# Cross-attention on one core: the score matrix A built from 11 block products of 64 rows, whose blocks VectorE adds, in place of 12

## The chip, the core and the metric

The kernel runs on one core of a Trainium2 chip. The metric is the device time of one execution in microseconds (us), the median of several runs. TensorE (PE in the profile) multiplies matrices into PSUM banks, VectorE (DVE) and ScalarE (ACT) read PSUM, GpSimd (POOL) works on SBUF, and SyncE (SP) issues the transfers. The order of the instructions on each engine is written out by hand: every engine does its work in the order in which the program names it, and waits where an operand is not ready.

## The reference

x has 16 batches of 256 rows and 256 columns, the context c 16 batches of 77 rows and 192 columns. There are 8 heads. All numbers are float32.

```
Q = x @ Wq,  K = c @ Wk,  V = c @ Wv          (8 heads of 256)
score = Q K^T / sqrt(256), masked             (16 x 8 x 256 x 77)
attn  = softmax(score)
out   = concat over heads (attn V) @ Wo + x
out   = layernorm(out) * gamma + beta
```

## The kernel before

The projections are folded. Once, at the start, the kernel forms for each head G = Wk Wq^T / 16 (192 x 256, in tiles gA for the first 128 context columns and gB for the other 64) and U = Wv Wo (tiles uA, uB). For a group of four batches and a pair of heads it then needs A = G^T c^T (256 x 77 for each head and batch, tile a), and for each batch VW = c U (tile vw). The scores of 128 rows of x (a "tile" t, two for each batch) are x A, and the output is attn VW.

A is prepared two heads at a time by `prepare_a` (L165): part A multiplies with the 128 context rows of gA and cA (L190), part B with the 64 rows of gB and cB, two heads at once on the two halves of the array's rows (L202). Four PSUM banks of 308 columns hold the result, and ScalarE copies them to SBUF (`copy_out`, L966). Seen in 64 rows of context, half of the 256 output rows (dc) and two of the four batches, a head takes 3 x 2 x 2 = 12 block products.

The main loop (L980) runs over batches; in iteration b it makes the scores of batch b+1 (L300), the softmax of it, the product attn VW of batch b, and the layer norm of batch b-1:

- TensorE: scores of two tiles; in every second iteration (those with odd b) the preparation of VW for two batches and of A for two pairs of heads; then `seven(b)` (L435 to L474), the product attn VW by seven block products.
- VectorE: `shift` (L317, adds the bias and takes the minimum, 16 instructions), the second normalisation of the older batch, a transposition, `finish` (L505, L508) and the reciprocals (L353), the first normalisation (L547, L576), `turn` (L369), the transposition of x (L162), and `add_product` (L497), which adds the product in PSUM to x.
- ScalarE: 16 exponentials (L338), the copies of VW and A (L966), the two small steps of `spread` (L526, L527) that give the norm's factor rstd, and the copy of four of the seven products (L473).
- GpSimd: `weigh` (L359), `differences` (L412), `sums` (L429 to L432) and `add_seven` (L483). At the start it also makes the bias (L596 to L598), the sums of uA and uB (L905, L906) and small copies (L638, L642, L643).

All PSUM tiles share one ring of eight banks: a new tile takes the bank of the tile eight places earlier, and its first matmul waits until that one's reader is done.

One row in the profile with "x32" counts 32 matmul instructions: each float32 matmul of the program is two instructions, and four of 32 output columns run side by side in the array, so that 8 instructions of 128 rows, or 16 of 64 rows, are one step of the stream.

Of the kernel before, what the change touches and what calls it, by code (L numbers as in the profile page):

```python
# [16 lines left out]
P = 128  # L17
H = 8
# [9 lines left out]
def kernel(  # L28
# [78 lines left out]
    bet = const.tile([P, DI], F32, tag="bet", name="bet")  # L107
    xg_of = {}

    x_rows = x.rearrange("b (t p) d -> p (b t) d", p=P)  # L110
# [8 lines left out]

    def load_x(g, n=None, of=QT):  # L120
        if not n:
            xg_of[g] = const.tile([P, GT, DI], F32, tag=f"xg{g}", name=f"xg_{g}")
        lo, hi = (0, GT) if n is None else (n * QT, n * QT + of)
        nc.sync.dma_start(xg_of[g][:, lo:hi], x_rows[:, g * GT + lo : g * GT + hi, :])

# [15 lines left out]

    def load_xT(g, lo=0, hi=GT, after_pool=False):


        if lo == 0:
            xT_of[g] = in_two("xT", [P, GT * NM, 2, BK], g)
        if after_pool:
            nc.gpsimd.memset(xT_of[g][:BK, lo * NM, 0, :1], 0.0)
        rows = x.rearrange("b s d -> (b s) d")[(g * GT + lo) * P : (g * GT + hi) * P, :]
        rows = rows.rearrange("(m r) (i n) -> i r m n", r=BK, i=NM)  # L150
        for i in range(NM):
            nc.sync.dma_start(
                xT_of[g][i * BK : (i + 1) * BK, lo * NM : hi * NM].rearrange(
                    "p m n q -> p m (n q)"
                ),
                rows[i],
            )

    def transpose_x(g, j):

        cols = xT_of[g][:, j * NM : (j + 2) * NM]
        nc.vector.transpose(cols, cols)  # L162


    def prepare_a(g, places, lo=0, hi=GB, rest_first=False):  # L165
# [46 lines left out]

        return part_A, part_B, copies

    def prepare_vw(b, rest_first=False):
# [77 lines left out]
    def scores(t):  # L293
        g = t // GT
        j, bl = t % GT, (t // QT) % GB
        ps = [ps_mm.tile([P, 512], F32, tag="mm", name=f"ps_{t}_{a}") for a in range(2)]
        for m in range(NM):
            for dc in range(2):
                for i in range(NM):
                    nc.tensor.matmul(  # L300
                        ps[m // 2][i * BK : (i + 1) * BK, m % 2 * 2 * S2 : (m % 2 + 1) * 2 * S2],
                        xT_of[g][:, j * NM + m, dc],
                        flat(a_of[g][:, dc, bl, 2 * i : 2 * i + 2, :]),
                        start=(dc == 0),
                        stop=(dc == 1),
                    )
        ps_of[t] = ps
# [24 lines left out]
    def exponential(t):  # L332
        e = sp.tile([P, H, S2], F32, tag="e", name=f"e_{t}")
        s, top = s_of.pop(t)
        den = st.tile([P, H], F32, tag="den", name=f"den_{t}")
        for h in range(H):
            one = slice(h, h + 1)
            nc.scalar.activation(  # L338
                e[:, h],
                s[:, h],  # L340
                AF.Exp,
                bias=top[:, one],
                scale=-1.0,
                accum_out=den[:, one] if summed_by_act(t) else None,
            )
        e_of[t] = e, den

# [128 lines left out]
    def add_seven(b):  # L476

        m = m_of.pop(b)
        j = QT * b % GT
        y = xg_of[QT * b // GT][:, j : j + QT].rearrange("p t (c d) -> p t c d", c=2)  # L480

# [13 lines left out]
    def add_product(t):  # L495
        y = xg_of[t // GT][:, t % GT, :]
        nc.vector.tensor_tensor(y, po_of.pop(t), y, ALU.add)  # L497

    def finish(t):
        if t in po_of:  # L500
            add_product(t)
        g, j = t // GT, t % GT
        y = xg_of[g][:, j, :]
        bn = st.tile([P, 6], F32, tag="bn", name=f"bn_{t}")
# [5 lines left out]
    def finish_halves(t):  # L510
        g, j = t // GT, t % GT
        bn = st.tile([P, 2, 6], F32, tag="bn2", name="bn_halves", bufs=1)
        for c, po in enumerate(po_of.pop(t)):
            y = xg_of[g][:, j, c * P : (c + 1) * P]
            nc.vector.tensor_tensor(y, po, y, ALU.add)
            nc.vector.bn_stats(bn[:, c], y)
# [28 lines left out]
    def centre(t):  # L545
        y = xg_of[t // GT][:, t % GT, :]
        nc.vector.scalar_tensor_tensor(  # L547
# [3 lines left out]
    def store(t):  # L551
        nc.sync.dma_start(out_rows[:, t, :], xg_of[t // GT][:, t % GT, :])

    def scale_and_store(t):
# [3 lines left out]
        rstd, _ = rstd_of.pop(t)  # L558
        y = xg_of[t // GT][:, t % GT, :]
        nc.scalar.activation(y, y, AF.Identity, scale=rstd)  # L560
# [3 lines left out]
    def normalise(t, aside=False, centred=False):  # L564

        g, j = t // GT, t % GT
        rstd, less = rstd_of.pop(t)
        y = xg_of[g][:, j, :]
        if aside:
# [11 lines left out]
        if t ^ 1 in done:  # L581
            t |= 1
            j |= 1
            nc.sync.dma_start(
                out_rows[:, t + 1 - QT : t + 1, :], xg_of[g][:, j + 1 - QT : j + 1, :]
            )

# [14 lines left out]
    with tc.tile_pool(name="wonce", bufs=1) as wp:  # L602
# [54 lines left out]

        qT_03 = const.tile([P, 2, 4, DI], F32, tag="xg0", name="qT_03")
        qT_12 = const.tile([P, 2, 4, DI], F32, tag="xg1", name="qT_12")
        kT_03 = const.tile([P, 2, 4, DL], F32, tag="xg2", name="kT_03")  # L660
        kT_12 = const.tile([P, 2, 4, DL], F32, tag="xg3", name="kT_12")
        qT = qT_03[:, 0].rearrange("p (e dc) d -> p e dc d", e=2)
        kT = kT_03[:, 0].rearrange("p (e dc) l -> p e dc l", e=2)
        qT_blk = {1: qT_12[:, 0], 2: qT_12[:, 1], 3: qT_03[:, 1]}
        kT_blk = {1: kT_12[:, 0], 2: kT_12[:, 1], 3: kT_03[:, 1]}
        for a in range(1, NF):
# [22 lines left out]
        def load_late():  # L689
# [3 lines left out]
            for a in range(NF):  # L693
                nc.sync.dma_start(wo_of[a // 2][:, a % 2], wo_rows[a])
            load_xT(0, 0, QT)
            load_bias(0, GB)
            load_rest()
            load_xT(0, QT, GT)
            load_bias(GB, B)
# [22 lines left out]
        def turn_k():  # L722
            pt = ps_mm.tile([P, 4, P], F32, tag="mm", name="pt_k")
            for n in range(4):
                nc.tensor.transpose(pt[:, n], wk_nat[:, n * P : (n + 1) * P], ident)
            nc.scalar.copy(kT_03[:, 0, :, :P], pt)

# [161 lines left out]
        for a in range(1, NF):  # L889
# [18 lines left out]
        for j in range(NF // 2):  # L908
# [3 lines left out]
            if j:  # L912
                transpose_x(0, 0)
                bias_of(0, GB)
# [36 lines left out]


    def work_of(b, rest_first=False):
        g, n = b // GB + 1, b % GB
        work = [prepare_vw(b, rest_first)]
        if g < NG - 1 or g == NG - 1 and n < NF // 2:
            work.append(prepare_a(g, (n,), rest_first=rest_first))
        elif b <= NS:
            part = (0, 2) if g < NG else (2, GB)
# [10 lines left out]
    def turn_x_and_normalise(g, n, old):  # L970
        to_turn = (g, 0) if g < NG and n == 2 else (g - 1, GT // 2) if g > 1 and n == 0 else None
        if to_turn:
            for j in range(to_turn[1], to_turn[1] + GT // 2, 2):
                transpose_x(to_turn[0], j)
        if old:
# [4 lines left out]
    for b in range(-1, B - 1):  # L980
# [17 lines left out]
        works = work_of(b + 1) if alone or n % 2 == 0 else []  # L998
        for part_A, _, _ in works:
            part_A()  # L1000
        for _, part_B, _ in works:
            part_B()
        if b == B - 2:
# [17 lines left out]
        for i, t in enumerate(new if b >= 0 else ()):  # L1021
# [3 lines left out]
            weigh(t)  # L1025
        ahead = works and not alone
        if old and not ahead:
            spread(old[0], old[-1] + 1)
        if ahead:
            copy_out(works)  # L1030
            if old:
                spread(old[0], old[-1] + 1)
            works = work_of(b + 2, rest_first=True)
            for _, part_B, _ in works:
                part_B()
            for part_A, _, _ in works:
                part_A()
        copy_out(works)
        if b + 1 < NS:
            differences(b + 1)  # L1040
        if ahead and g < NG:
            load_xT(g, n * QT, (n + 1) * QT, after_pool=True)
        if b < NS:
            if now:
                seven(b)
            if old:
                invert(old[0], old[-1] + 1)
                normalise(old[0])
            for t in new:
                turn(t)  # L1050
            if b < 0:
                for j in range(QT, GT, 2):
                    transpose_x(0, j)
                bias_of(GB, B)
            if alone or ahead:
                turn_x_and_normalise(g, n, old)
                if ahead and g < NG:
                    load_xT(g, (n + 1) * QT, (n + 2) * QT)
            else:
# [61 lines left out]
```

## Time and profile before

| what | value |
|---|---|
| median of 3 runs | 270.72 us (270.66 to 272.16) |
| profiled execution, first to last instruction (span) | 269.2 us |
| what lies around the span, median less span | 1.5 us |
| TensorE busy | 262.9 us, 98% of the span |
| GpSimd busy | 173.2 us, 64% |
| VectorE busy | 185.2 us, 69% |
| ScalarE busy | 157.7 us, 59% |
| granted TensorE clock | 1.000 over the span |

No separate time of the profiled execution itself is given beside its span, so sums that are made in the span are set against the median by the 1.5 us around it. "Busy" is the share in which at least one instruction of the engine ran; idle time of an engine costs something only where another one waits for it.

### The profile page before, as it was taken

The numbers are of one execution on the slowest core, as the hardware profiler recorded it, in microseconds if no ns is written. First come the engines' busy times: TensorE is split into PE (matmuls) and PEld (weight loads), VectorE is DVE, ScalarE is ACT, GpSimd is POOL, SyncE is SP. The second block draws the span as 40 slices with busy tenths as digits, with TensorE's granted clock in tenths as the row PEclk, the third lists the DMA queues.
The fourth block names the chain that finished last, engine by engine and source line by source line (L and its number), as shares of the span: only waits on it lengthen the run. The fifth ranks groups of instructions, "written<-read, shape, count | busy, mean of one in ns | idle before, by whom it ended". The sixth has DMA issues, their size and how long they took to land.

```text
span 269.2 us, 14427 instructions
## 1 busy us (share of the span) xinstructions
PE 262.9 (98%) x6090; PEld 194.3 (72%) x6090; DVE 185.2 (69%) x808; ACT 157.7 (59%) x667; POOL 173.2 (64%) x240
## 2 busy tenths in 40 slices
PE   8999999999999999999999999999999999999993
PEld 7566598954985599459954995499769967984662
DVE  1555966483574758764896379647977897799785
ACT  3243335626857555964587377738684595636772
POOL 1042005637399647995699759965999799685462
PEclk9999999999999999999999999999999999999999
DMA  6999999901500130323022400340044010100112
GB/s 193 200 204 206 325 144 171 322 9 32 130 7 2 41 82 5 69 82 94 5 62 70 110 6 14 108 123 4 6 119 122 2 44 5 44 22 22 44 41 80
DMA packets 41616, 22.69 MB, mean 84 GB/s; under 512 B 24064, under 2 KB 40528, under 8 KB 41552
## 3 DMA queue, kind: packets, MB, share of 16 engines
q1 hardware_dynamic: 41168, 20.98, 32.7%
q0 software_dynamic: 384, 0.79, 1.4%
q8 instruction: 48, 0.79, 1.2%
q14 instruction: 16, 0.13, 0.2%
HBM read 17.57 MB, written 4.19 MB: 81 GB/s over the span
## 4 chain that ended last, share of the span: by engine, by line
PE 93%; DMA 3%; DVE 1%; SPq 1%; issue 0%; DVEq 0%
PE ps L300 25%; PE pa L190 12%; PE pv L224 11%; PE po L448 11%; PE pm L448 8%; PE pa L202 6%; PE pv L235 6%; PE po L381 4%; PE pu L777 3%; PE pr L260 2%; PE pgb L838 2%; DMA c_sb<-in_ctx_dram 2%; DMA wk_blk<-in_L_xattn_Wk_dram 2%; PE pw L791 1%; PE phb L854 1%; PE pr L271 1%
## 5 line engine op out<-in xcount | busy, mean ns | idle before, releaser
L338 ACT ACTIVATE e<-s,top 128x77 f32<-128x77 f32 x256 | 85.3, 346 | 44.5 <-DVE top L317 38.2
L300 PE MATMUL ps<-a,xT 128*32 128x154 f32 x2048 | 70.1, 294 | 0.0
L300 PEld LDWEIGHTS ps<-a,xT 128*32 128x32 f32 x2048 | 66.5, 110 | 1.1 <-issue 0.4
L359 POOL TENSOR_TENSOR p<-e,rden 128x512 f32<-128x512 f32 x64 | 47.5, 768 | 29.5 <-DVE rden L353 29.4
L317 DVE CUSTOM_DVE_ANT_0 s<-ps,bias 128x77 f32<-128x77 f32 x256 | 43.6, 232 | 14.8 <-PE ps L300 14.8
L338 ACT ACTIVATION_READ_ACCUMULATOR e<-s,top 128x1 f32 x224 | 42.0, 187 | 0.0
L190 PE MATMUL pa<-cA,gA 128*32 128x308 f32 (+1 forms) x576 | 36.8, 395 | 0.0
L190 PEld LDWEIGHTS pa<-cA,gA 128*32 128x32 f32 x576 | 19.0, 110 | 20.4 <-issue 6.7
L483 POOL TENSOR_TENSOR xg<-xg,m 128x256 f32<-128x256 f32 x39 | 28.7, 736 | 6.6 <-DVE xg L497 4.6
L576 DVE SCALAR_TENSOR_TENSOR xg<-xg,rstd,bet 128x256 f32<-128x256 f32 x27 | 22.2, 821 | 14.7 <-ACT rstd L527 13.3
L224 PE MATMUL pv<-uA,cA 128*32 128x512 f32 x256 | 30.8, 595 | 0.0
L412 POOL TENSOR_TENSOR ts<-vw 128x768 f32<-128x768 f32 x13 | 24.0, 1848 | 5.9 <-ACT vw L966 5.9
L369 DVE STREAM_TRANSPOSE pT<-p 128x640 f32<-128x640 f32 x32 | 25.5, 820 | 3.4 <-POOL p L359 3.3
L966 ACT COPY vw<-pv 128x512 f32<-128x512 f32 x32 | 17.8, 584 | 15.3 <-PE pv L224 8.1
L497 DVE TENSOR_TENSOR xg<-po,xg 128x256 f32<-128x256 f32 x31 | 11.5, 405 | 14.5 <-PE po L448 13.9
L317 DVE DVE_READ_ACCUMULATOR2_ANT top<- 128x1 f32 x256 | 20.8, 81 | 0.0
L202 PE MATMUL pa<-cB,gB 64*32 64x308 f32 (+2 forms) x512 | 20.4, 387 | 0.0
L966 ACT COPY a<-pa 128x308 f32<-128x308 f32 (+1 forms) x56 | 18.9, 395 | 1.9 <-PE pa L190 0.4
L202 PEld LDWEIGHTS pa<-cB,gB 64*32 64x32 f32 (+1 forms) x512 | 11.0, 110 | 11.4 <-issue 6.2
L547 DVE SCALAR_TENSOR_TENSOR xg<-xg,mv,gam 128x256 f32<-128x256 f32 x30 | 17.5, 585 | 0.1
L235 PE MATMUL pv<-uB,cB 64*32 64x512 f32 x256 | 17.3, 597 | 0.0
L224 PEld LDWEIGHTS pv<-uA,cA 128*32 128x32 f32 x256 | 8.0, 109 | 12.5 <-issue 9.5
(119 smaller groups left out, 407.6 us busy)
## 6 DMA issues: line engine op xcount, KB each, us to landing
xT<-in_x_dram SPq DMA_DIRECT2D x52, 64.0 KB, 2.4
xg<-in_x_dram SPq DMA_DIRECT2D x6, 512.0 KB, 4.2
out_dram<-xg SPq DMA_DIRECT2D x11, 256.0 KB, 2.3
wo<-in_L_xattn_Wo_dram SPq DMA_DIRECT2D x4, 512.0 KB, 8.9
wq_blk<-in_L_xattn_Wq_dram SPq DMA_DIRECT2D x12, 128.0 KB, 4.5
out_dram<-xg SPq DMA_DIRECT2D x10, 128.0 KB, 1.7
wk_blk<-in_L_xattn_Wk_dram SPq DMA_DIRECT2D x12, 96.0 KB, 4.3
xg<-in_x_dram SPq DMA_DIRECT2D x1, 1024.0 KB, 7.9
```

The source lines that it names most:

```text
L190: nc.tensor.matmul(flat(o[i * BK : (i + 1) * BK]), gA[:, h, cols(dc, i)], flat(cA[:, batches, :]), start=not rest_first and n in opening, ...
L202: nc.tensor.matmul(flat(banks[j + k][i * BK : (i + wide) * BK]), gB[half(k), h // 2, dc * P + i * BK : dc * P + (i + wide) * BK], flat(cB[ ...
L224: nc.tensor.matmul(pv[k][i * BK : (i + 1) * BK], cA[:, b, k * BK : (k + 1) * BK], uA[:, parts, :, i], start=not rest_first, stop=rest_first,)
L235: nc.tensor.matmul(pv[k][i * BK : (i + 1) * BK], cB[half(k), b, k * BK : (k + 1) * BK], uB[half(k), parts, :, i], start=rest_first, stop=n ...
L300: nc.tensor.matmul(ps[m // 2][i * BK : (i + 1) * BK, m % 2 * 2 * S2 : (m % 2 + 1) * 2 * S2], xT_of[g][:, j * NM + m, dc], flat(a_of[g][:, ...
L317: nc.vector.tensor_tensor_reduce(s[:, h], ps[a][:, k * S2 : (k + 1) * S2], bias[:, b, :], scale=-1.0, scalar=FAR, op0=ALU.add, op1=ALU.min ...
L338: nc.scalar.activation(e[:, h], s[:, h], AF.Exp, bias=top[:, one], scale=-1.0, accum_out=den[:, one] if summed_by_act(t) else None,)
L359: nc.gpsimd.tensor_tensor(part, e_mh[:, :, :, keys], rden_mh.unsqueeze(3).to_broadcast(list(part.shape)), ALU.mult,)
L369: nc.vector.transpose(pT_of[t].rearrange("p n m q -> p m n q"), p.rearrange("p m (n k) -> p m n k", k=BK),)
L448: nc.tensor.matmul(out[i * BK : (i + 1) * BK], weight[:, i], moving, start=first and n == 0, stop=final and n == len(terms) - 1,)
L483: nc.gpsimd.tensor_tensor(to, to, what, ALU.add)
L966: nc.scalar.copy(dst, src)
```

## The change

For the pairs of heads of groups 1 and 2 and two of the four pairs of group 3 (ten pairs, prepared in iterations b = -1, 1, 3, 5 and 7, where `quick` is true), `prepare_a` is replaced by `prepare_fast`. Of the three blocks of 64 context rows the first two are multiplied by a scheme of seven block products in place of eight (sums of blocks of G and c take the place of the blocks); the third block adds four more. Each is a product of 64 rows and 154 columns, and two heads' products run at once on the two halves of the rows: 11 such steps for a pair of heads.

- The sums of the blocks are made once by GpSimd: `sums_of_g` after the last pair of G, 14 instructions of 64 partitions and 512 elements; `sums_of_c(1, 2)` ahead of the sum of uB; `differences_of_c` and `sums_of_c(2, 4)` after the first two `weigh`.
- For each head one bank "mids" and one bank "ends" of three times 154 columns. The first product of a "mids" bank is copied by ScalarE, and the next product is added onto it in the same place. VectorE then puts the blocks together by four additions that read PSUM (`put_together`); ScalarE no longer copies these parts of A.
- In a quick iteration TensorE makes both batches' VW first (both parts A, then both parts B), then the two pairs of heads, then `seven`. VectorE's additions stand after the two `turn` and ahead of the transposition of x and the second normalisation. The first `put_together` is ahead of the second `turn`.
- The tiles of x (xg) and of the turned x (xT) hold two batches and not four, x in a ring of four and xT in a ring of three, and the exponentials are written in place of the shifted scores. The order of their transfers is the same. The K weights that are turned at the start share the space of the sums of G.

The parts of the diff that the prediction speaks of (the rest changes only the names of the smaller tiles):

```diff
+    HB = GB // 2
+    KX = HB * S2
+    FAST = NG - 1
+    low, high = slice(0, LB), slice(LB, P)
+    cT = const.tile([P, 4, FAST, KX], F32, tag="cT", name="cT")
+    cD = const.tile([P, FAST, KX], F32, tag="cD", name="cD")
+    gC = const.tile([P, NF, P], F32, tag="gC", name="gC")
...
+    def load_x(k):
+        xg_of[k] = const.tile([P, PT, DI], F32, tag=f"xg{k % 4}", name=f"xg_{k}")
+        nc.sync.dma_start(xg_of[k], x_rows[:, k * PT : (k + 1) * PT, :])
...
+            xT_of[k] = pools[0].tile([P, PT * NM, 2, BK], F32, tag="xT", name=f"xT_{k}", bufs=3)
...
+    def sums_of_g():
+        parts = gA.rearrange("p (u e) (i dc c) -> p dc e u i c", e=2, dc=2, c=BK)
+        sums = gS.rearrange("p n (u e) (i c) -> p n e u i c", e=2, c=BK)
+        for e, own, other in ((0, high, low), (1, low, high)):
+            s1, s2, s3 = (sums[own, n, e] for n in range(3))
+            s4 = sums[other, 0, e]
+            nc.gpsimd.tensor_copy(s1, parts[other, 1, e])
+            add(s1, s1, parts[own, 1, e])
+            subtract(s2, s1, parts[own, 0, e])
+            subtract(s3, parts[own, 0, e], parts[own, 1, e])
+            nc.gpsimd.tensor_copy(s4, s2)
+            subtract(s4, parts[other, 0, e], s4)
+            nc.gpsimd.tensor_copy(gC[own], gB[other, :, P:])
+    def halves_of(c, lo, hi):
+        groups = c[:, lo * GB : hi * GB].rearrange("p (g y b) k -> p y g (b k)", y=2, b=HB)
+        return groups[:, 0], groups[:, 1]
+    def sums_of_c(lo, hi):
+        xs, ys = halves_of(cA, lo, hi)
+        t1, t2, t3, t4 = (cT[:, n, lo - 1 : hi - 1] for n in range(4))
+        subtract(t1, ys, xs)
+        for own, other in ((low, high), (high, low)):
+            nc.gpsimd.tensor_copy(t2[own], ys[other])
+        subtract(t3, t2, ys)
+        subtract(t2, t2, t1)
+        for own, other in ((low, high), (high, low)):
+            nc.gpsimd.tensor_copy(t4[own], t2[other])
+        subtract(t4, xs, t4)
+    def differences_of_c(lo, hi):
+        subtract(cD[:, lo - 1 : hi - 1], *halves_of(cB, lo, hi))
...
+    def prepare_fast(g, u):
...
+        for e, h in enumerate(heads):
+            for banks in (mids, ends):
+                banks.append(ps_mm.tile([P, 3, KX], F32, tag="mm", name=f"pf_{g}_{h}_{len(ends)}"))
...
+        def middle(e):
+            h, own = heads[e], (high, low)[e]
+            return [
+                ((mids[e], 2), from_g(own, h, 0), c_of(cA, own, xs)),
+                ((mids[e], 0), from_s(own, 0, h), t_of(own, 0)),
+                ((mids[e], 2), from_s(own, 1, h), t_of(own, 1)),
+                ((mids[e], 1), from_s(own, 2, h), t_of(own, 2)),
+                (
+                    (mids[e], 1),
+                    lambda i: gC[own, u, i * BK : (i + 1) * BK],
+                    c_of(cB, own, ys),
+                ),
+            ]
+        def outer(e):
+            h, own = heads[e], (low, high)[e]
+            return [
+                ((ends[e], 0), from_g(own, h, 0), c_of(cA, own, xs)),
+                ((ends[e], 1), from_s(own, 0, h), c_of(cA, own, ys)),
+                ((ends[e], 2), from_g(own, h, 1), t_of(own, 3)),
+                ((ends[e], 0), from_rest(h, 0), c_of(cB, own, xs)),
+                ((ends[e], 1), from_rest(h, 0), c_of(cB, own, ys)),
+                ((ends[e], 2), from_rest(h, 1), cD[own, g - 1]),
+            ]
+        def pairs():
+            o, m = outer(0), middle(1)
+            ones = o[:2] + m[:1] + o[2:] + m[1:]
+            o, m = outer(1), middle(0)
+            return list(zip(ones, m[:1] + o[:3] + m[1:] + o[3:]))
+        def products():
+            total = {id(bank): 6 for bank in ends} | {id(bank): 5 for bank in mids}
+            lone = {id(bank): e for e, bank in enumerate(mids)}
+            seen = dict.fromkeys(total, 0)
+            for pair in pairs():
+                flags = []
+                for (bank, _), _, _ in pair:
+                    key = id(bank)
+                    n, seen[key] = seen[key], seen[key] + 1
+                    one = key in lone and n == 0
+                    flags.append(
+                        (one or n == (key in lone), one or n == total[key] - 1, one)
+                    )
+                for i in range(NM):
+                    for ((bank, n), weight, moving), (start, stop, _) in zip(pair, flags):
+                        nc.tensor.matmul(
+                            bank[i * BK : (i + 1) * BK, n],
+                            weight(i),
+                            moving,
+                            start=start,
+                            stop=stop,
+                        )
+                for ((bank, n), _, _), (_, _, one) in zip(pair, flags):
+                    if one:
+                        nc.scalar.copy(blocks[lone[id(bank)]][:, 0], by_batch(bank)[:, n])
+        def plus(out, *of):
+            nc.vector.tensor_tensor(out, *of, ALU.add)
+        def put_together(e):
+            mid, end, of = by_batch(mids[e]), by_batch(ends[e]), blocks[e]
+            plus(of[:, 3], mid[:, 2], of[:, 0])
+            plus(of[:, 1:3], mid[:, 0:2], of[:, 3:4].to_broadcast([P, 2, HB, S2]))
+            plus(of[:, 3], mid[:, 0], of[:, 2])
+            plus(of[:, 0:3], end, of[:, 0:3])
+        return products, put_together
...
-        e = sp.tile([P, H, S2], F32, tag="e", name=f"e_{t}")
...
-                e[:, h],
+                s[:, h],
...
+        gS = const.tile([P, 3, H, P], F32, tag="gS", name="gS")
+        sums_of_g()
         load_x(0)
+        load_x(1)
         nc.sync.dma_start(gam, gamma.partition_broadcast(P))
...
         turn_rest_last()
+        sums_of_c(1, 2)
         sum_of(uB)
         for t in range(QT):
             exponential(t)
             weigh(t)
+        differences_of_c(1, NG)
+        sums_of_c(2, NG)
...
+    def fast(b):
+        return b < B - GB - GB // 2
...
-            load_x(g, n, 2 * QT)
+            load_x((g * GB + n) // 2)
...
+        ahead = not alone and n % 2 == 0
+        quick = ahead and fast(b + 1)
...
+        if quick:
+            works += work_of(b + 2)
+            for part_A, *_ in works:
+                part_A()
+            for _, part_B, _ in works:
+                part_B()
+            copy_out(works[:1])
+            products, put_together = prepare_fast(g, n)
+            products()
+            copy_out(works[1:])
...
+        if quick:
+            if old:
+                spread(old[0], old[-1] + 1)
+            if b < 0:
+                for t in new:
+                    turn(t)
+                for t in range(QT, GT, 2):
+                    transpose_x(t)
+            next_products, next_together = prepare_fast(g, n + 1)
+            next_products()
...
+            elif not quick:
+                for t in new:
+                    turn(t)
+            if quick:
+                for e, t in enumerate(new):
+                    if b >= 0:
+                        turn(t)
+                    put_together(e)
+                for e in range(2):
+                    next_together(e)
```

More of the change, by code (lines that the diff above doesn't have):

```diff
@@ L118, in half, with x_of @@
         return slice(i * LB, (i + 1) * LB)
[L120 to L124, printed above, removed]
+    def load_x(k):
+        xg_of[k] = const.tile([P, PT, DI], F32, tag=f"xg{k % 4}", name=f"xg_{k}")
+        nc.sync.dma_start(xg_of[k], x_rows[:, k * PT : (k + 1) * PT, :])
+    def x_of(t, n=1):
+        return xg_of[t // PT][:, t % PT : t % PT + n]
     evacs = [0]
@@ L213, in prepare_a @@
         return part_A, part_B, copies
+    add, subtract = (
+        partial(nc.gpsimd.tensor_tensor, op=op) for op in (ALU.add, ALU.subtract)
+    )
[12 more added lines that the diff above has]
+            nc.gpsimd.tensor_copy(gC[own], gB[other, :, P:])
@@ L656, in pair_in_order @@
             return parts[::-1] if a == 1 else parts
[L658 to L665, printed above, removed]
+        qT_blk = [const.tile([P, 4, DI], F32, tag=f"xg{a}", name=f"qT_{a}") for a in range(NF)]
+        kT_all = const.tile([P, NF, 4, DL], F32, tag="gS", name="kT_all")
+        kT_blk = [kT_all[:, a] for a in range(NF)]
+        qT = qT_blk[0].rearrange("p (e dc) d -> p e dc d", e=2)
+        kT = kT_blk[0].rearrange("p (e dc) l -> p e dc l", e=2)
         for a in range(1, NF):
@@ L725, in turn_k @@
                 nc.tensor.transpose(pt[:, n], wk_nat[:, n * P : (n + 1) * P], ident)
-            nc.scalar.copy(kT_03[:, 0, :, :P], pt)
+            nc.scalar.copy(kT_blk[0][:, :, :P], pt)
         def turn_k_last():
@@ L955, in work_of @@
         work = [prepare_vw(b, rest_first)]
-        if g < NG - 1 or g == NG - 1 and n < NF // 2:
-            work.append(prepare_a(g, (n,), rest_first=rest_first))
-        elif b <= NS:
+        if b <= NS and not fast(b):
             part = (0, 2) if g < NG else (2, GB)
@@ L997 @@
         alone = b + 1 >= B - GB // 2
[L998 to L1002, printed above, removed]
+        ahead = not alone and n % 2 == 0
+        quick = ahead and fast(b + 1)
+        works = work_of(b + 1) if alone or ahead else []
+        if not quick:
+            for part_A, *_ in works:
+                part_A()
+            for _, part_B, _ in works:
+                part_B()
         if b == B - 2:
@@ L1025 @@
             weigh(t)
[L1026 to L1030, printed above, removed]
+        if quick:
+            works += work_of(b + 2)
+            for part_A, *_ in works:
+                part_A()
+            for _, part_B, _ in works:
+                part_B()
+            copy_out(works[:1])
+            products, put_together = prepare_fast(g, n)
+            products()
+            copy_out(works[1:])
+        elif not alone or old:
+            if ahead:
+                copy_out(works)
             if old:
                 spread(old[0], old[-1] + 1)
[L1033 to L1038, printed above, removed]
+            if ahead:
+                works = work_of(b + 2, rest_first=True)
+                for _, part_B, _ in works:
+                    part_B()
+                for part_A, *_ in works:
+                    part_A()
+        if not quick:
+            copy_out(works)
+        if quick:
[8 more added lines that the diff above has]
+            next_products()
         if b + 1 < NS:
@@ L1048 @@
                 normalise(old[0])
-            for t in new:
-                turn(t)
             if b < 0:
-                for j in range(QT, GT, 2):
-                    transpose_x(0, j)
                 bias_of(GB, B)
+            elif not quick:
[8 more added lines that the diff above has]
+                    next_together(e)
             if alone or ahead:
```

81 lines of the change are left out of this document (51 added, 30 removed).

## The prediction, made before the result was known

> **What bounds the kernel now.** I read the page's first part, then the chain of waits, then the timeline of VectorE over one pair of iterations, then the sums by stretch of time.
>
> ```profile
> PE 262.9 (98%) x6090; PEld 194.3 (72%) x6090; DVE 185.2 (69%) x808; ACT 157.7 (59%) x667; POOL 173.2 (64%) x240
> ```
>
> TensorE is busy for nearly the whole span. The chain of waits (start, length, engine, tile and line, number of instructions) says the same: from 13 to 264 us it never leaves TensorE for long. These are rows of it, among them the quick iteration b = 3, which starts at 104.09.
>
> ```profile
> 28.34 1.04 PE pa L202 x16
> ...
> 46.83 5.82 PE pr L260 x32
> ...
> 55.66 1.85 PE pv L224 x16
> ...
> 71.66 1.75 PE pm L448 x64
> ...
> 104.09 4.19 PE ps L300 x128
> 108.28 1.72 PE pv L224 x16
> 110.00 2.07 PE pa L190 x32
> 112.07 1.02 PE pv L235 x16
> 113.09 1.04 PE pa L202 x32
> 114.13 0.86 PE pv L235 x16
> 114.99 1.04 PE pa L202 x32
> 116.02 1.85 PE pv L224 x16
> 117.88 2.07 PE pa L190 x32
> 119.95 1.75 PE pm L448 x64
> 121.70 2.17 PE po L448 x64
> ...
> 187.74 4.19 PE ps L300 x128
> ```
>
> A pair of heads costs TensorE 2.07 + 1.04 = 3.11 us, and no row here waits for another engine. But how far is the next engine from being the bound? VectorE over the same stretch (start, length, line; in brackets the idle time before and what ended it):
>
> ```profile
> 106.90 0.22 DVE L317 CUSTOM_DVE_ANT_0 s<-ps,bias 128x77 f32<-128x77 f32 x1
> ...
> 115.99 0.64 DVE L576 SCALAR_TENSOR_TENSOR xg<-xg,rstd,bet 128x256 f32<-128x256 f32 x1 [2.58 <-ACT rstd L527]
> ...
> 119.70 0.84 DVE L576 SCALAR_TENSOR_TENSOR xg<-xg,rstd,bet 128x256 f32<-128x256 f32 x1
> 123.94 0.76 DVE L497 TENSOR_TENSOR xg<-po,xg 128x256 f32<-128x256 f32 x2 [3.40 <-PE po L448]
> 124.98 0.24 DVE L317 CUSTOM_DVE_ANT_0 s<-ps,bias 128x77 f32<-128x77 f32 x1 [0.29 <-PE ps L300]
> ...
> 134.13 0.72 DVE L497 TENSOR_TENSOR xg<-po,xg 128x256 f32<-128x256 f32 x2
> 134.78 0.22 DVE L317 CUSTOM_DVE_ANT_0 s<-ps,bias 128x77 f32<-128x77 f32 x1
> ```
>
> ```profile
> 104.09:131.98 27.89, 27.89 (x713) 20.23 (x708) 19.20 (x97) 18.16 (x82) 22.22 (x30) 1.00 0.23 60
> ...
> 187.74:212.58 24.84, 24.84 (x713) 20.18 (x708) 20.05 (x95) 16.83 (x82) 22.13 (x30) 1.00 0.25 67
> ```
>
> The first of these two rows (length, then busy time and instructions of PE, PEld, DVE, ACT and POOL) is a pair of iterations: 27.89 us, TensorE busy in all of it, VectorE in 19.20. So VectorE seems to have 8.7 us to spare. It has not: what counts is its own loop, from one first shift (L317) to the next. Only the 3.40 and the 0.29 us are waits for TensorE. The 2.58 us are a wait for ScalarE, which must first do 16 exponentials, copies and `spread`; a wait inside the order of the engine stays when work is put behind it. Without waits for TensorE the quick part runs from 106.90 to 120.54 (119.70 + 0.84) and 0.76 for L497: 14.4 us. The other part runs from 124.98 to 134.78, 9.8 us; there the shifts were spread out by TensorE's scores, and with these done early I take 9.5, since the exponentials, which set its length, stay. The loop is 14.4 + 9.5 = 23.9 us against 27.89. **VectorE's real slack is 4.0 us a pair of iterations.**
>
> **The change part by part.** *TensorE.* The new steps are those of part B on half the batches, 64 rows by 32 columns and 154 moving columns:
>
> ```profile
> 196.27 0.86 PE pv L235 x16
> 197.13 0.52 PE pa L202 x32
> ```
>
> 32 instructions are two steps, 0.26 us each. Eleven steps cost 2.88 us (at 0.262) in place of 3.11, which is 0.23 for a pair of heads and 2.3 us for the ten. The turns between 128 and 64 rows, some 0.15 us each (1.02 against 0.86, 1.85 against 1.72), are two a quick iteration as before. TensorE's own pair of iterations becomes 27.4 us. The price for 176 instructions on end is not shown, since 32 is the longest run of this shape: from below 0.26 a step; from above the pace of the densest long run, 64 instructions in the 1.75 us of L448, 27.3 ns each, which is 0.437 us a step of 16. I take 0.262, the row of the same shape. [...]
>
> *VectorE.* Each head adds four two-operand additions that read PSUM, of 154, 308, 154 and 462 columns, each using what the one before left except the last. The nearest rows by shape:
>
> ```profile
> L497 DVE TENSOR_TENSOR xg<-po,xg 128x256 f32<-128x256 f32 x31 | 11.5, 405 | 14.5 <-PE po L448 13.9 <-PE po L381 0.5
> ...
> L515 DVE TENSOR_TENSOR xg<-po,xg 128x128 f32<-128x128 f32 x2 | 0.6, 288 | 0.0
> ```
>
> 128 columns more cost 117 ns, 0.91 to 1.04 ns a column with some 0.16 us fixed. I get 0.31, 0.46, 0.31 and 0.61 = 1.69 us; independent neighbours overlap by some 0.08 us (two L497 take 0.76), dependent ones do not. I take 1.65 a head, with 1.5 (every start as close as two L497) and 1.85 (no overlap, a gap at each step) as ends. A quick iteration has four heads: **6.6 us more on VectorE (6.0 to 7.4), where the slack is 4.0.** ScalarE loses eight copies and gains four small ones. The factor rstd comes as late as before:
>
> ```profile
> 112.64 0.18 ACT L338 ACTIVATION_READ_ACCUMULATOR e<-s,top 128x1 f32 x1
> 113.18 1.07 ACT L966 COPY vw<-pv 128x512 f32<-128x512 f32 x2 [0.36 <-PE pv L235]
> ...
> 115.75 0.20 ACT L527 ACTIVATE rstd<-log 128x2 f32<-128x2 f32 x1
> ```
>
> Measured from the first shift S (106.90), the exponentials end at S + 5.9, two copies of VW at 7.0, two small copies at 7.5, two more of VW at 8.5, `spread` at 9.1; now it is 115.95 - 106.90 = 9.05. So VectorE's wait for rstd stays, and the new loop is 23.9 + 6.6 = **30.5 us a pair**, 3.1 over TensorE's 27.4.
>
> *How TensorE then waits.* A "mids" bank takes its second product in place only when ScalarE has copied the first. With TensorE ahead, step 6 of the first pair waits for that copy at S + 7.3. From there follow 6 steps (1.57), the second pair (2.88), a turn (0.15), `seven` (3.92), scores (4.19) and `seven` (3.92): the scores of the next quick iteration start at S + 23.9. The banks of `seven` and of the next scores are those that `put_together` sets free, at about S + 12 and later; that is in time. `seven(b+1)` needs sums made after the second `turn`, also in time.
>
> *The start.* GpSimd gets 6 copies and 8 additions of 512 elements between the last G (its matmuls end at 28.34, ScalarE's two copies by some 29.1) and the bias.
>
> ```profile
> L905 POOL TENSOR_TENSOR uA<-uA 128x512 f32<-128x512 f32 x1 | 1.3, 1280 | 0.0
> ...
> L760 POOL COPY cB<-cB 64x224 f32<-64x224 f32 x1 | 0.4, 368 | 8.2 <-DVE cB L133 8.2
> 40.70 0.20 POOL L596 TENSOR_TENSOR nan<-nan 128x4 f32<-128x4 f32 x1 [18.81 <-DVE nan L595]
> 45.48 0.36 POOL L638 COPY cRA<-cA 128x208 f32<-128x208 f32 x1 [0.92 <-DVE cA L637]
> 68.25 0.74 POOL L432 TENSOR_TENSOR ss<-pT,ss 128x256 f32<-128x256 f32 x1
> ```
>
> At 1.28 and some 0.6 us they take about 14 us and end at 43.4, not hidden in full by the idle 18.8 us: the queue behind 40.70 slips 2.7 us, the copy cRA ends at 47.6, and `prepare_last` (46.83) waits 0.9. The sums of c add some 3.8, 1.2 and 5.7 us (estimates from the same rows) in the queue ahead of `sums(0)`, which ends at 73.9 in place of 69.0; `seven(0)` (71.66) would wait for it 2.2 us. VectorE is as late by itself: with TensorE at 56.6 in place of 55.66, four rows of VW (5.3) and the first pair (2.9), the additions of b = -1 begin at 65.1 and end at 71.7, the first shift of b = 0.
>
> *The transfers.* SP's queue keeps its order. The tile of x for batches 8 and 9 now waits for the store of batches 0 and 1, issued in the same iteration b = 3, some five iterations before it is used; the writes of the turned x behind it are used two iterations later. I price that at nothing; the lead of 70 us covers it, and without it a whole transfer would show. In-place exponentials add no wait: `turn` already waits for the `weigh` that frees the tile.
>
> **The sum.** First shift of b = 0 at 71.7; of b = 1 at 71.7 + 9.5 = 81.2; three pairs later, b = 7 at 81.2 + 91.5 = 172.7. Scores of b = 9 then start at 172.7 + 23.9 = 196.6, where the chain before has 187.74: 8.9 us later. From there nothing is changed, and TensorE (24.84 us a pair by the second row of the sums) is again just over VectorE's loop of 23.9; I add 0.5 us for a bank set free late. That makes +9.4 us on the span of 269.2, 278.6, and 270.72 + 9.4 = **280.1 us** on the median.
>
> **The rivals.**
>
> - *TensorE stays the bound.* If the additions fall into VectorE's 8.7 idle us, only the 2.3 us come off: 268.4, faster. If in that case `seven(0)` still waits for GpSimd, it is 2.2 us at b = 0 and four gains of 0.46 behind it: 271.1, no change. For it: the 69% of VectorE. Against: each addition would have to take under 0.25 us (4.0 over 16), less than the smallest such row, 288 ns.
> - *TensorE's issue becomes the bound* (slower still). At 0.437 us a step a quick iteration costs TensorE 22 x 0.175 = 3.9 us more, 31.3 a pair, over VectorE's 30.5. Then the additions begin 11 steps later in b = -1 (+1.9), each of three pairs takes 0.8 more (+2.4), and behind the last wait 17 steps cost 3.0 more: 280.1 + 7.3 = 287.4 us. It decides from about 0.40 us a step. [...] Against: the 16 ns of the row.
> - *The change doesn't do what it says*, the two heads' steps running one behind the other: part B's row, two heads at once, speaks against it; it would look like the second rival, and I count it there.
>
> **How the numbers follow.** VectorE's loop 0.76, with 276 to 284 from its bounds (0.1 us more for a head is 0.4 in the loop and 1.6 at the end; the start gives a us either way). Issue-bound 0.10, 284 to 288. TensorE still the bound: faster 0.08, no change 0.06. A measurement tells 1%, 2.7 us, from no change. The range of 274 to 287 leaves out the third case, the top of the second and a little of the first. Faster 0.08, same 0.07, slower 0.85.
>
> **What would show it.** In the profile after: TensorE's share falls to about 94%, with three waits of some 3 us a piece at `prepare_fast` for a ScalarE copy, in b = 3, 5 and 7; VectorE's idle time for L497 and L317 behind TensorE is gone from b = 2 to 8, while its wait for rstd of some 2.5 us is still there; first shifts 30.5 us apart; a head's four additions take 1.65 us; steps of 0.26 us. `prepare_last` waits for cRA and `seven(0)` for the sums. If the first shifts stay 27.4 to 28 us apart, VectorE's slack was misjudged; if steps take 0.4 us without a wait, it was the issue.

## The result, and the profile after

The changed kernel takes **290.95 us** (290.75 to 291.06), the kernel before beside it 270.69: a ratio of 1.0743 [1.0716, 1.077], 20.3 us slower. The profiled execution took 291.06 us with a span of 289.2, where the forecast had 278.6. From the page, the busy times and the chain by engine:

```profile
PE 267.2 (92%) x7210; PEld 211.9 (73%) x7210; DVE 217.5 (75%) x888; ACT 148.0 (51%) x647; POOL 195.3 (68%) x271
...
PE 77%; DMA 12%; issue 6%; SPq 4%; DVE 1%; DVEq 0%
```

VectorE has its 32 us more, as the additions should cost. But the chain that ended last does not run through VectorE: 1% of it does. It is TensorE (the 12% of DMA lie at the start, before 48 us), and 6% "issue", time in which TensorE waited for nothing that the profile shows. Where that is, the chain tells by order of time in b = 3 (start, length, engine, tile and line, matmuls):

```profile
122.17 2.34 PE pf L351 x139
124.51 0.76 issue
125.27 2.39 PE pf L351 x126
127.66 1.19 issue
128.84 1.77 PE pf L351 x86
130.61 1.32 PE pm L606 x41
131.93 0.80 issue
```

The 22 new steps (`pf`) last from 122.17 to 130.61, 8.44 us, in place of the 5.76 of the sum: 0.38 us a step. 6.50 us of it are matmuls, 0.30 a step where 0.262 was forecast, and 1.95 are two stops, which are not in the forecast at all. The five quick iterations (b = -1 to 7) spend 8.7, 9.0, 8.4, 9.4 and 10.4 us in these steps, so b = 3 is the mildest. Between the stops stand 126 matmuls, and between the second and the next one, in `pm`, 86 + 41 = 127. Waits, summed by engine and what ended them (total us, times, longest), show that this is all the waiting `prepare_fast` does, and that the three waits of some 3 us for a ScalarE copy, which the forecast named as its sign, are absent:

```profile
PE pf L351 <- issue: 12.3, 10, 2.2
...
PE pr L419 <- POOL cRA L792: 1.0, 1, 1.0
```

Sums by stretch, in the columns of the prediction: a pair of iterations from the scores of iteration b = 3 to those of b = 5, and one after the last quick iteration:

```profile
112.67:143.87 31.20, 28.46 (x937) 24.71 (x931) 25.37 (x113) 16.23 (x78) 22.07 (x30) 1.00 0.20 54
207.58:232.42 24.84, 24.84 (x710) 20.78 (x705) 19.95 (x95) 16.81 (x82) 22.06 (x30) 1.00 0.24 67
```

The pair takes 31.20 us, in which TensorE is idle for 2.74. VectorE is busy for 25.37 of it, where it had 19.20 of 27.89: 6.2 us more. The second row is as before. VectorE's timeline over the same iteration:

```profile
115.45 0.22 DVE L476 CUSTOM_DVE_ANT_0 s<-ps,bias 128x77 f32<-128x77 f32 x1
...
124.77 0.48 DVE L733 SCALAR_TENSOR_TENSOR xg<-xg,rstd,bet 128x256 f32<-128x256 f32 x1 [2.81 <-ACT rstd L684]
...
136.87 0.24 DVE L476 CUSTOM_DVE_ANT_0 s<-ps,bias 128x77 f32<-128x77 f32 x1
```

From first shift to first shift this is 21.4 us (forecast 14.4 + 6.6 = 21.0), and the wait for rstd of 2.8 us stayed. So VectorE's loop is as long as forecast, and yet the time is 10.6 us longer. Both engines are near a bound here, and only experiments can say which of them does what.

### The profile page after: what moved, and what is told of

It is laid out like the page before. It is cut to its first block, busy times and chain, and to the rows that moved or that the text cites. A ratio compares the mean times of both kernels' runs of the same rounds, so it can differ in the third digit from the quotient of the medians.

```text
span 289.2 us, 16834 instructions
## 1 busy us (share of the span) xinstructions
PE 267.2 (92%) x7210; PEld 211.9 (73%) x7210; DVE 217.5 (75%) x888; ACT 148.0 (51%) x647; POOL 195.3 (68%) x271
## 4 chain that ended last, share of the span: by engine, by line
PE 77%; DMA 12%; issue 6%; SPq 4%; DVE 1%; DVEq 0%
PE ps L459 22%; PE pf L351 12%; PE po L606 10%; PE pv L383 10%; PE pm L606 8%; PE pv L394 5%; PE po L539 4%; DMA wo<-in_L_xattn_Wo_dram 3%; DMA wvT<-in_L_xattn_Wv_dram 3%; PE pr L419 2%; DMA wk_blk<-in_L_xattn_Wk_dram 2%; DMA wq_blk<-in_L_xattn_Wq_dram 2%; SPq L164 2%; DMA wq_nat<-in_L_xattn_Wq_dram 2%; PE pa L202 1%
## 5 line engine op out<-in xcount | busy, mean ns | idle before, releaser
L496 ACT ACTIVATE s<-s,top 128x77 f32<-128x77 f32 x256 | 85.3, 346 | 50.6 <-DVE top L476 41.8
L517 POOL TENSOR_TENSOR p<-s,rden 128x512 f32<-128x512 f32 x64 | 47.6, 770 | 29.3 <-DVE rden L511 29.2
L496 ACT ACTIVATION_READ_ACCUMULATOR s<-s,top 128x1 f32 x224 | 41.9, 187 | 0.0
L363 DVE TENSOR_TENSOR a<-pf,a 128x154 f32<-128x154 f32 x80 | 34.1, 434 | 4.3 <-PE pf L351 1.6
L351 PE MATMUL pf<-cT,gS 64*32 64x154 f32 x480 | 20.7, 305 | 1.4 <-issue 1.4
L631 ACT COPY m<-pm 128x512 f32<-128x512 f32 x13 | 7.5, 576 | 27.4 <-PE pm L606 27.4
L351 PE MATMUL pf<-cB,gB 64*32 64x154 f32 x320 | 18.4, 304 | 2.3 <-issue 2.3
L640 POOL TENSOR_TENSOR m<-m 128x128 f32<-128x128 f32 x26 | 11.9, 459 | 12.2 <-ACT m L631 11.2
L351 PEld LDWEIGHTS pf<-cT,gS 64*32 64x32 f32 x480 | 16.7, 111 | 4.1 <-issue 4.0
L606 PE MATMUL po<-vr,pT 128*32 128x256 f32 x208 | 17.8, 379 | 0.0
```

Source lines behind the costliest of these rows:

```text
L351: nc.tensor.matmul(bank[i * BK : (i + 1) * BK, n], weight(i), moving, start=start, stop=stop,)
L363: nc.vector.tensor_tensor(out, *of, ALU.add)
L496: nc.scalar.activation(s[:, h], s[:, h], AF.Exp, bias=top[:, one], scale=-1.0, accum_out=den[:, one] if summed_by_act(t) else None,)
L517: nc.gpsimd.tensor_tensor(part, e_mh[:, :, :, keys], rden_mh.unsqueeze(3).to_broadcast(list(part.shape)), ALU.mult,)
L606: nc.tensor.matmul(out[i * BK : (i + 1) * BK], weight[:, i], moving, start=first and n == 0, stop=final and n == len(terms) - 1,)
L640: nc.gpsimd.tensor_tensor(to, to, what, ALU.add)
```

## The experiments

**Three kernels that take the two suspects apart.** The theory: TensorE's instructions reach it in blocks (126 and 127 matmuls between the stops of b = 3, each with its weight load, from one start to the next 3.57 and 3.89 us), and the narrow steps use them up faster than they come. The rival is the forecast's own loop of VectorE. The first kernel halves TensorE's instructions in the steps by weights of 64 columns in place of 32 (G is stored with the halves of its columns outermost, so that two blocks of 32 lie side by side); the columns that move through the array, and VectorE's work, are the same:

```diff
-                for i in range(NM):
+                for i in range(0, NM, 2):
...
-            return lambda i: gA[rows, h, (2 * i + dc) * BK : (2 * i + dc + 1) * BK]
+            return lambda i: gA[rows, h, dc * P + i * BK : dc * P + (i + 2) * BK]
```

> The changed kernel with weights of 64 columns in place of 32 in the eleven steps (G is stored with its two halves of columns one after the other, so that they lie side by side): the same products, half the TensorE instructions of a step, 88 for a pair of heads in place of 176. Theory I (TensorE's instructions arrive in blocks of 256, one each 3.6 to 4 us, and the steps use one up in 2.1 us): the stretches of issue time in the two pairs of heads go, the stage falls from 8.4 to 10.4 us to under 7, and only VectorE's loop of some 31 us a pair of iterations is left: 281 to 283 us in place of 290.95. Theory V (VectorE's loop alone is the bound, and TensorE's stops only fill its waits): within 1 us of 290.95. Theory W (the loading of weights is what is slow): no gain or slower, as the same columns are loaded.

The second leaves TensorE as it is and puts one copy in place of VectorE's four additions for each head (the sums are left out, so A is not A); the third does both:

```diff
-            plus(of[:, 3], mid[:, 2], of[:, 0])
-            plus(of[:, 1:3], mid[:, 0:2], of[:, 3:4].to_broadcast([P, 2, HB, S2]))
-            plus(of[:, 3], mid[:, 0], of[:, 2])
-            plus(of[:, 0:3], end, of[:, 0:3])
+            nc.vector.tensor_copy(of[:, 1:4], end)
```

> The changed kernel with the four additions of each head replaced by one copy of the bank of ends to SBUF (462 columns, some 0.6 us): it leaves out three additions and one operand of the fourth, so A is not A; TensorE, ScalarE and GpSimd have the same work. VectorE's loop falls from 31 to some 26.5 us a pair of iterations. Theory V: TensorE's own 27.4 us is the bound again, 272 to 274 us. Theory I: the stops of issue time stay, 2.7 to 4.6 us in each quick iteration, and with them 30 to 32 us a pair of iterations: 285 to 290 us.

> Both at once: weights of 64 columns, and one copy in place of each head's four additions (A is not A). Both theories: TensorE is the bound with some 27.5 us a pair of iterations, and only the start's wait for GpSimd is left: 271 to 274 us. If it stays over 278, there is a third bound.

| kernel | us | ratio to before |
|---|---|---|
| changed | 290.95 | 1.0743 [1.0716, 1.077] |
| wide weights | 281.91 | 1.041 [1.0374, 1.0447] |
| no additions | 288.87 | 1.0701 [1.0648, 1.0754] |
| both | 271.67 | 1.0023 [1.0003, 1.0044] |

Wide weights alone give back 9.0 us; the additions alone only 2.1; both 19.3. Two bounds stand one behind the other, and one of them hides most of the other. The chain of the first kernel in b = 3 shows the second bound undisturbed:

```profile
112.98 4.30 ACT s L496 x25
117.27 0.95 ACT vw L1126 x2
118.22 0.19 ACT a L360
...
118.46 4.94 PE pf L351 x142
```

```profile
PE pf L351 <- ACT a L360: 7.6, 4, 2.4
```

No stop is left in the steps (142 of 176 matmuls in 4.94 us, 0.278 us a step of 8), and now TensorE waits for ScalarE's small copy, as the forecast said: four times, 1.9 us on average, where it had three waits of some 3. The first shifts of b = 0, 1 and 7 in VectorE's timeline:

```profile
71.77 0.23 DVE L476 CUSTOM_DVE_ANT_0 s<-ps,bias 128x77 f32<-128x77 f32 x1
...
80.85 0.22 DVE L476 CUSTOM_DVE_ANT_0 s<-ps,bias 128x77 f32<-128x77 f32 x1
...
172.32 0.22 DVE L476 CUSTOM_DVE_ANT_0 s<-ps,bias 128x77 f32<-128x77 f32 x1
```

They are within 0.4 us of the forecast's 71.7, 81.2 and 172.7, and (172.32 - 80.85) / 3 = 30.49 us apart. Its profiled span is 278.7. The forecast was thus the time of a kernel whose instructions come in time. Its median, 281.91, is 1.8 us above the forecast of 280.1, and that goes with the granted clock: the profiled execution had 0.998 and took 280.45, the three others had 0.986 or 0.987 and took 281.63 to 282.44.

In the second kernel the stops stay where they were, and the additions' place is free:

```profile
120.49 2.35 PE pf L351 x142
122.84 0.73 issue
123.57 2.33 PE pf L351 x127
125.90 1.45 issue
```

In the third, the steps run on end but for one stop of 1.1 us in the whole run, and TensorE is the bound again (97% of the span):

```profile
104.22 4.19 PE ps L456 x128
...
113.72 5.92 PE pf L351 x176
...
131.81 4.19 PE ps L456 x128
```

A pair of iterations takes 27.59 us there (131.81 - 104.22) against 27.89 before. That is all that eleven steps in place of twelve are worth, with everything else taken away: 0.3 us a pair.

**Weights of 128 columns** (the same edit with i + 4, two calls for each step; 44 matmuls a pair of heads).

> The changed kernel with weights of 128 columns, one matmul in place of four in each product: 44 TensorE instructions for a pair of heads in place of 176. If a step keeps its 0.262 us, the same as with 64 columns, 281 to 283 us, bound by VectorE's loop. Theory W: loading 128 columns takes 187 ns where two steps' worth of matmuls take 131, so a step takes 0.37 us and the stage 8.2 us; then TensorE is level with VectorE's loop and the time 283 to 287 us.

It took 282.39 us (1.044 [1.0419, 1.0462]), no better than the 281.91 us with 64 columns: half as many matmuls gave nothing more, and VectorE's loop is what is left. Theory W does not hold: in b = -1, at a granted clock of 1.00, the 88 matmuls take 6.02 us, 0.27 us a step. In b = 3 a step took 0.38 us, but there the granted clock was 0.74.

**The rest of the change without the scheme.** `fast(b)` is false, so that `prepare_a` makes all of A; the tiles of two batches and the exponentials in place remain, the sums of G and c are left out.

> The changed kernel's tiles of two batches for x and turned x, and exponentials in place, but A by prepare_a everywhere as before, and no sums of G and c. All theories: these parts cost nothing, 270.0 to 271.5 us. If the smaller tiles or the in-place exponentials make a wait, it shows here alone.

Measured: 270.77 us, 1.000 [0.9981, 1.0018]. The transfers cost nothing, as taken.

**The same with the sums**, which GpSimd makes and nobody reads.

> The changed kernel with A by prepare_a everywhere, but with all sums of G and c still made by GpSimd and used by nobody: the price of the start alone. Prediction's step: the product of batch 0 waits some 2.2 us for sums(0) behind GpSimd's queue, prepare_last waits 0.9 us for cRA, and nothing later makes it up: 272.7 to 273.5 us against 270.8 without the sums. If the sums are hidden: 270.8.

Measured: 271.83 us, 1.0044 [1.0026, 1.0061], and `prepare_last` waits 1.4 us for GpSimd, for cRA. The start costs 1.1 us, less than expected: the first shift of b = 1 came at 78.54 in place of 77.67.

**Stops in the kernel before.** If narrow steps are enough to make stops, they must come without the scheme too. A's matmuls of the whole groups are cut, part A into four of 77 columns and part B into two of 154, 192 matmuls for a pair of heads in place of 64. (The cut matmuls take the context of batches 0 to 3 for every group, so the scores of the later groups are not the reference's.)

> The kernel before, with no block products, no sums and no additions: only the matmuls of A in the main loop's whole groups are cut along the 308 moving columns, part A into four of 77 and part B into two of 154. The same columns pass the array and the weights' order is the same; VectorE, ScalarE and GpSimd have the work of before; a pair of heads takes 192 TensorE matmul instructions in place of 64 (176 in the changed kernel). Theory I (blocks of 256 instructions, one each 3.6 to 4 us): 256 instructions more than before for the two pairs of a quick iteration need at least 3.6 us more of supply; issue time appears in the stage, 2 to 6 us in each of the iterations b = -1, 1, 3, 5, 7: 281 to 300 us. Without theory I: 271 to 273 us. Theory W (loading each instruction's weights is slow) would show as steps that are slower throughout and no stretches of issue time.

It took 278.26 us, 1.0302 [1.0264, 1.034]. The chain has a stop, in the middle of part B:

```profile
117.29 0.57 PE pa L206 x33
117.86 0.98 issue
118.84 0.76 PE pa L206 x31
```

So stops come without the scheme, with nothing changed but the size of the matmuls. Of the 7.7 us that it took longer, 4.2 are six such stops, in part B and behind it in `pm` and `po`; the other 3.5 are a busier TensorE (266.4 us against 262.9). The stops cost less than expected: I had counted each block of the stretch as late, and one is late here.

**A mixed version**: one pair of heads in each quick iteration by the scheme (wide weights), the other by `prepare_a`, to have VectorE's additions within its slack of 4 us. Two orders were tried, both with GpSimd's sums of only half the heads and those of c moved to its idle time: `prepare_a` first, with b = 1 to 7 quick, and the scheme first, with b = -1 to 7 quick. From the edit of the first:

```diff
-            copy_out(works[:1])
-            products, put_together = prepare_fast(g, n)
+            copy_out(works[:2])
+            if old:
+                spread(old[0], old[-1] + 1)
+            copy_out(works[2:])
+            products, put_together = prepare_fast(g, n + 1)
...
-            next_products, next_together = prepare_fast(g, n + 1)
-            next_products()
```

> A version built on what was found: 11 steps with weights of 64 columns for one pair of heads in each of the quick iterations b = 1, 3, 5 and 7, and prepare_a for the other pair and for b = -1; the sums are made for these heads alone and those of c are moved to where GpSimd waits. VectorE's loop becomes 23.9 + 3.3 = 27.2 us a pair of iterations, TensorE's 27.66: TensorE stays the bound and four times 0.23 us come off. 269.7 to 270.2 us against 270.8; if VectorE's loop is 0.5 us longer than that, 270.8 to 272.

> A second version of one pair of heads in each quick iteration (b = -1, 1, 3, 5, 7), in another order: both batches' VW, then the 11 steps with weights of 64 columns, and prepare_a for the other pair last, so that ScalarE's copy of the first product stands ahead of the four copies of the other pair and spread comes as early as before. Sums for these heads alone (7 us of GpSimd in its idle time at the start), those of c where GpSimd waits. VectorE's loop 20.7 + 9.75 - 3.3 = 27.2 us a pair of iterations, TensorE's 27.66, GpSimd hidden: five times 0.23 us come off, 269.4 to 270.0 us against 270.7. If ScalarE's copy or VectorE is late again by a little, 270.5 to 272.

The first took 274.95 us (1.0172 [1.0147, 1.0196]). The chain shows a wait that I had not priced: the small copy that the scheme needs stands on ScalarE behind VW's and A's copies.

```profile
117.58 1.29 ACT a L1123 x4
...
119.28 0.96 ACT vw L1123 x2
120.24 0.20 ACT a L356
```

The second took 272.91 us (1.0091 [1.0075, 1.0108]). In a middle pair of iterations (sums by stretch, then the chain) TensorE is busy for the whole of it, and it still isn't faster:

```profile
133.16:161.16 28.00, 28.00 (x736) 21.47 (x732) 23.27 (x105) 17.58 (x81) 22.84 (x30) 1.00 0.21 61
```

```profile
142.66 3.07 PE pf L351 x88
```

88 matmuls, the eleven steps of one pair, took 3.07 us against the 3.11 of `prepare_a`. There is nothing to win with them. Of the 2.3 us that are lost, 1.6 are waits of TensorE for the additions, in two other iterations:

```profile
PE pm L606 <- DVE a L363: 1.6, 2, 1.3
```

No version here beats the kernel before.

**The supply measured by itself.** Behind the last product of the kernel before stand three runs of matmuls, on operands that lie ready, with 24 loads of x issued ahead of them:

```diff
+    burst("narrow", 128, 2, 1)
+    burst("long", 32, 4, 1)
+    burst("wide", 32, 2, 2)
```

The numbers are steps, batches of 77 moving columns, and blocks of 32 columns of weights.

> The kernel before, with three runs of matmuls put behind its last product, on operands that lie ready and into banks that nobody reads: 2048 matmul instructions of 64 rows by 32 columns with 154 moving columns (the shape of the new steps), then 512 of the same with 308 moving columns, then 256 with weights of 64 columns and 154 moving ones. Nothing in them waits for another engine. For the first 10 us the other engines finish their work and hardly anything is transferred; then 6 MB of x are loaded into a buffer that is no longer used. Its span says nothing about the kernel; what counts is the pace inside. If instructions arrive in blocks of 256 every 3.6 to 4.0 us, the first run goes at 128 matmuls in 3.6 to 4.0 us with stops between blocks, 58 to 64 us in all, from its first blocks on and also without transfers; the second and the third need 4.2 to 4.5 us for 128 by themselves and have no stop. If blocks come late only while transfers share the queues, the first 10 us go at 2.3 us for 128 and the stops come with the loads. If the stops belong to something in the changed stage (its banks, its copies), there are none, and the first run takes 37 us.

The chain over the three (tile names are those of the runs):

```profile
264.05 3.54 PE narrow L1097 x203
267.59 1.60 issue
269.19 2.33 PE narrow L1097 x128
...
273.47 6.16 PE narrow L1097 x256
...
318.23 1.68 issue
319.91 2.33 PE narrow L1097 x128
322.24 1.16 issue
...
324.64 16.95 PE long L1097 x506
341.59 8.54 PE wide L1097 x256
```

The narrow run stops first after 203 matmuls, and then goes 128 matmuls, stops, 128 matmuls, stops, to its end. The one exception is the run of 256: in its 6.16 us the granted clock was 0.60 and then 0.85, and no stop stands between the two blocks; with the stop of 1.02 us behind them they took 3.6 us each. The 2048 matmuls take 60.5 us (264.05 to 324.5), 3.8 us for 128, where 2.33 are work. With 308 moving columns (4.2 us for 128, 16.95 x 128 / 512) and with wide weights (4.3 us) there is no stop. And the transfers of the stretch 317 to 324 us (GB/s in 40 slices, then packets and MB in all and by queue) hold nothing else than the instructions themselves:

```profile
GB/s 94 0 0 0 0 0 0 0 0 0 0 0 0 0 0 0 0 0 0 0 0 0 94 0 0 0 0 0 0 0 0 0 0 0 0 0 0 0 0 0
DMA packets 2, 0.03 MB, mean 5 GB/s; under 512 B 0, under 2 KB 0, under 8 KB 0
...
q8 instruction: 2, 0.03, 2.1%
```

Two packets of 16 KB on the queue "instruction", 22 slices of 0.175 us, 3.85 us apart, and two stops of 1.68 and 1.16 us. The stops of this stretch are not contention with other transfers, since there are none; while x was loaded at 150 GB/s (the loads came with the run, sooner than I had expected) they were 1.0 to 2.2 us, hardly other. The whole executions give the same count: 57 packets (0.93 MB, 16 KB each) for the 7210 matmuls of the changed kernel, 48 for the 6090 of the kernel before, 70 for the 8906 of this run, about 127 matmuls to a packet, with as many weight loads. A block of 128 with the stop behind it took 3.45 to 4.55 us in this run, 2.33 of them work. What sets this time, and when a packet is asked for, no run here shows.

## Why the prediction was wrong, point by point

- **TensorE's step of 0.262 us: the step that failed.** The price came from 32 instructions on end, and the prediction said that a long run was not shown, with 0.437 as the other end. Inside a block a step takes 0.29 us (2.33 x 16 / 128 in the measured run), a tenth more; with wide weights it takes 0.27 to 0.28. Over the whole stage, stops included, it took 0.38 us in b = 3 and up to 0.47 in b = 7. Of the 10.9 us between forecast and median (290.95 less 280.1), the wide weights, which take the stops away, give back 9.0. The rival "TensorE's issue becomes the bound" was the right one: the stage of 22 steps at 0.437 is 9.6 us, and the five measured 8.4 to 10.4. But its mechanism was thought of as a pace of each instruction. What the runs show is stops between blocks: the 32 instructions of the price ran on end in 0.52 us, 16 ns each, and the narrow run stopped first after 203 and then behind each 128 but one. A slow pace of each is not what acted: 128 matmuls in 2.33 us are 18 ns each, for 128 on end, where 0.437 us a step is 27.
- **The rival's 287.4 us was too low by 3.6.** Stops also fall behind the steps (0.80 in `pm` above), and in b = 7 the clock fell. Two first shifts of the changed kernel, b = 1 and b = 7:

```profile
82.60 0.24 DVE L476 CUSTOM_DVE_ANT_0 s<-ps,bias 128x77 f32<-128x77 f32 x1 [0.43 <-PE ps L459]
...
178.04 0.22 DVE L476 CUSTOM_DVE_ANT_0 s<-ps,bias 128x77 f32<-128x77 f32 x1
```

  Against the forecast the first came 1.4 us late (81.2), three pairs of iterations took 95.4 us in place of 91.5 (+3.9), and from there to the scores of b = 9, at 207.58, it was 29.5 in place of 23.9 (+5.6). That is 10.9 in all, and the span missed by 10.6. The rival had +1.9, +2.4 and +3.0 for these three parts. Of the last part some 1.5 us go with the clock and not with the supply: in the steps of b = 7 (sums by stretch) the granted clock was 0.84, and the matmuls took 8.02 us in place of the 6.46 of b = 1 at 1.00.

```profile
184.78:195.20 10.42, 8.02 (x357) 6.88 (x344) 6.79 (x16) 2.83 (x9) 7.66 (x10) 0.84 0.28 80
```

  Why the clock fell there, no run here shows.
- **VectorE's slack of 4.0 us and its loop of 30.5 us: right**, shown by the wide weights (30.5 apart, span 278.7 against 278.6). That the sum fits so closely is partly luck: around b = 3 the loop's two parts are 20.7 and 9.75 us, where the prediction had 21.0 and 9.5, and in the first the wait for rstd is 1.8 us in place of 2.6 while the additions cost more. The four additions cost somewhat more than the 1.65 us a head. By form (count, busy us, mean ns) they are 0.64 + 2 x 0.31 + 0.48 = 1.74:

```profile
L363 DVE TENSOR_TENSOR a<-pf,a 128x462 f32<-128x462 f32 x20 | 12.8, 640 | 1.4
L363 DVE TENSOR_TENSOR a<-pf,a 128x154 f32<-128x154 f32 x40 | 12.3, 309 | 2.2 <-PE pf L351 1.6
L363 DVE TENSOR_TENSOR a<-pf,a 128x308 f32<-128x308 f32 x20 | 9.6, 479 | 0.7
```

- **TensorE's wait for ScalarE's copy: right in mechanism, hidden in the changed kernel**, where the stops make TensorE later than the copy. It is there as soon as the stops are gone.
- **The gain of 2.3 us on TensorE** (0.23 a pair of heads): too high. The third kernel had 0.30 us for two pairs of heads, which is 1.5 for ten.
- **The start**: cRA's wait was 1.0 us against 0.9 forecast. The sums by themselves cost 1.1 us at the end; the 2.2 us for `seven(0)` are not among the waits of the changed kernel, where TensorE came to `seven(0)` only at 75.39 and GpSimd had ended `sums(0)` at 73.15.
- **The transfers at nothing, and the pace of 24.84 us from b = 9 on: right.**

## What to carry to other kernels

Count the instructions of a stage against its time, not only its columns: in the supply measured by itself, matmuls that took 2.33 us for 128 (256 instructions with their loads) had a stop of 1.0 to 2.2 us behind the first 203 and then behind each 128 but one, and matmuls that took 4.2 or 4.3 us for 128 had none; "issue" in the chain with runs of 128 between was the sign. The cure here was fewer and larger instructions for the same work, weights of 64 columns in place of 32, which gave back 9.0 us. And before a scheme that saves one product in twelve is worth its additions, ask what is the saving in the engine's own time (0.3 us of 27.9), and how much room the other engine has in its own loop, not in its share of the span.

## What was not expected of the hardware

The instruction supply: the page had it all along as a row of the queues, 48 packets before and 57 after, 1.2% and 1.4% of the time of the 16 DMA engines, which I had passed over.

```profile
q8 instruction: 48, 0.79, 1.2%
...
q8 instruction: 57, 0.93, 1.4%
```

The kernel before uses 713 matmuls in 27.89 us, a packet in 5.0 us on average, and has no stop in its quick iterations. The changed one uses 937 in 31.2, one in 4.3; but in the steps it is one in 2.1 to 2.3 us (223 matmuls in 3.66 us in b = 5, 128 in 2.33), and the average says nothing of that.
